# Regrouping an attention loop: four tensor bursts a batch instead of eight

## The chip, the cores and the metric

The kernel runs on one core of one Trainium2 chip. The metric is the device time of one execution in microseconds (us).

The engines are called TensorE (PE in the profile; PEld is its weight load), VectorE (DVE), ScalarE (ACT), GpSimd (POOL) and SyncE (SP).

## The reference

There are 32 batches of 512 x 512 floats and one 512 x 512 adjacency. Layer 0 is a graph sum with two weight matrices and a layer norm. Layer 1 is masked attention with 8 heads of 64 and a layer norm.

```
# layer 0
mi, mj = x @ Wi.T, x @ Wj.T
x = layernorm(x + deg * (mi + b) + adj @ mj)
# layer 1, 8 heads of 64
q, k, v = x @ Wq.T + bq, x @ Wk.T + bk, x @ Wv.T + bv
scores = q @ k.T / 8;  scores[adj == 0] = -inf
x = layernorm(x + (softmax(scores) @ v) @ Wo.T + bo)
```

## The kernel before

All matmuls of 512 columns in float32 show as two instructions. On the whole array one of these takes 0.43 us (eight in 3.43 us, from 2054.74 to 2058.17 in the trace of the kernel before); eight of the scores, two heads at once, take 1.92 us (2079.41 to 2081.33). Two heads form a pair (`hp`), four pairs make a batch, and the 512 keys are four blocks (`kc`). Scores use the upper and the lower half of the array for the two heads at once (64*128 in the profile), values and denominators its left and right half (128*64), everything else the whole array (128*128).

```
def scores(b, hp, kc):
    ps = sc_tile()                                   # PSUM, 2 tiles of 2 banks
    for s in range(2):                               # two heads, one in each row half
        nc.tensor.matmul(ps[:, s, :], KT..., QT..., start=True, stop=True)
    e = E[kc] = work([P, 2, N], "e", 4)
    nc.scalar.activation(e, ps, AF.Exp)
    nc.vector.tensor_tensor(e, e, edge..., op=OP.mult)        # the mask product
    ... nc.vector.tensor_add(ES[hp], ES[hp], e)               # sum over key blocks

def values(b, hp, half): ...   # E[kc] times V, two key blocks, into PV[hp]
def sums(b, hp): ...           # ones times ES: the denominators
def invert / scale: ...        # VectorE: reciprocal in two halves, check, OT = PV * rl
```

A burst of attention is such a run of scores, values and denominators with nothing between them. The other work of a batch is a list `todo` of pieces, which belong to the next batch's layer 0 and its q, k, v and to the last batch's projection. The loop puts it between the bursts of attention. In the traces VectorE and ScalarE work in the order in which the program issues it (kernel before, from 2079 to 2098 us).

```
for step in range(8):
    hp, half = divmod(step, 2)
    scores(b, hp, 2 * half); scores(b, hp, 2 * half + 1)
    values(b, <pair and half of the step before>)     # and sums(), if it was a second half
    ... an eighth of todo, with invert, invert, scale put between its pieces
```

Pieces:

```
def l0_gather(b, dc):              # four of them open a batch
    pt = mm_tile()                 # mm: two PSUM banks, shared by all pieces in turn
    ... 4 transposes of x into pt
    nc.vector.tensor_mul(XD[b][:, dc, :], pt, deg_r)
    pm = mm_tile()
    # x = xhi + xlo: xhi is cast by ScalarE, xlo = x - xhi comes from VectorE
    ... 4 matmuls of xhi, then 4 of xlo, into pm
    nc.scalar.copy(AX_T[b][:, dc, :], pm)

def l0_out(b, ic):                 # bias on VectorE, 8 matmuls, ln_apply(ic - 1), sum, statistics
def l0_norm(b, ic):                # 4 transposes of the normed rows, ScalarE takes them out
```

## Time and profile before

| | before |
|---|---|
| time, median of the 3 runs before the prediction | 4282.94 us (4280.12 to 4285.44) |
| TensorE busy | 97% |
| VectorE, ScalarE, GpSimd busy | 61%, 21%, 9% |
| granted TensorE clock, mean | 0.996 |
| first scores of batch 0 | 112.4 us after the start |
| batch 0, mean of batches 1 to 30, last batch | 121.95, 131.79, 94.87 us |

The last two rows are read from the start of the first scores of each batch. They add up to the span: 112.4 + 121.95 + 30 x 131.785 + 94.87 = 4282.8 us. A difference in the mean of batches 1 to 30 counts 30 times.

The view of waits of the kernel before, TensorE only (who waited, for whom, us in total, times, longest):

```profile
PE mm L205 <- DVE xlo L182: 32.4, 32, 3.9
PE mm L205 <- ACT l L211: 23.8, 93, 0.3
PE mm L246 <- DVE xh L224: 10.7, 31, 0.3
```

TensorE waits about 0.9 us a batch for xlo, three times 0.24 us for ScalarE's copies between the gathers, and 0.34 us for VectorE once before the v matmuls. These are its only regular waits.

### The profile page before, as it was taken

Reading aid. Unit: us, or ns where it says so; the run is one execution under the profiler, and the core shown is the slowest. Engines: PE = TensorE matmul, PEld = TensorE weight load, DVE = VectorE, ACT = ScalarE, POOL = GpSimd, SP = SyncE. Lnnn points to the kernel's source line nnn. Section 1 sums busy time; section 2 is a strip of 40 time slices with the busy share of each in tenths; the row PEclk is TensorE's granted clock in tenths of the full one; section 3 lists DMA queues with packets and bytes.
Section 4 is the critical chain, followed back from the end, with each engine's and each line's share of the span. In section 5 each row is a group of like instructions: output and inputs, shape, how many; then the busy total and the mean of one; then the engine's idle time right before and its main releaser. Section 6 shows DMA issues by size and latency. Waiting matters only on the chain.

```text
span 4282.8 us, 31600 instructions
## 1 busy us (share of the span) xinstructions
PE 4174.9 (97%) x12826; PEld 1789.9 (42%) x12826; DVE 2607.0 (61%) x3081; ACT 894.1 (21%) x1159; POOL 399.1 (9%) x654
## 2 busy tenths in 40 slices
PE   8999999999999999999999999999999999999997
PEld 4444444444444444444444444444444444444442
DVE  2566566666566655566656666656665556665667
ACT  1222221122212222212222112221222221222211
POOL 1010001100011000111000110001100011100011
PEclk9999999999999999999999999999999999999999
DMA  2000000000000000000000000000000000000000
GB/s 106 0 20 20 1 20 20 20 20 1 20 20 20 20 19 1 20 20 20 20 1 20 20 20 20 1 20 20 20 20 20 1 20 20 20 20 1 20 10 20
DMA packets 37941, 77.29 MB, mean 18 GB/s; under 512 B 1248, under 2 KB 1248, under 8 KB 37792
## 3 DMA queue, kind: packets, MB, share of 16 engines
q1 hardware_dynamic: 35376, 70.26, 4.7%
q10 hardware_dynamic: 2112, 4.19, 0.3%
q8 instruction: 101, 1.65, 0.2%
q0 software_dynamic: 304, 0.79, 0.1%
q14 instruction: 48, 0.39, 0.0%
HBM read 41.68 MB, written 33.55 MB: 18 GB/s over the span
## 4 chain that ended last, share of the span: by engine, by line
PE 91%; DVE 6%; ACT 2%; issue 1%; DMA 0%; POOL 0%; ACTq 0%
PE mm L220 21%; PE mm L262 11%; PE sc L273 11%; PE mm L246 10%; PE mm L254 10%; PE mm L318 10%; PE ov L290 9%; PE mm L205 6%; DVE e L277 2%; PE ov L297 2%; ACT l L211 1%; PE mm L236 1%; ACT e L276 1%; DVE es L280 1%; DVE xh L224 1%
## 5 line engine op out<-in xcount | busy, mean ns | idle before, releaser
L277 DVE TENSOR_TENSOR e<-e,edge 128x1024 f32<-128x1024 f32 x512 | 680.7, 1350 | 999.4 <-ACT e L276 999.4
L276 ACT ACTIVATE e<-sc 128x1024 f32<-128x1024 f32 x512 | 496.3, 1021 | 1551.4 <-PE sc L273 1551.4
L273 PE MATMUL sc<-q,k 64*128 64x512 f32 x2048 | 510.6, 617 | 0.0
L290 PE MATMUL ov<-e,v 128*64 128x512 f32 x2048 | 496.8, 605 | 6.3 <-DVE e L277 3.8
L262 PE MATMUL mm<-l,wk 128*128 128x512 f32 x1024 | 466.7, 599 | 0.0
L318 PE MATMUL mm<-wo,oT 128*128 128x512 f32 x1024 | 460.0, 602 | 5.6 <-DVE oT L311 5.6
L246 PE MATMUL mm<-wv,l 128*128 128x512 f32 x1024 | 453.7, 596 | 11.4 <-DVE xh L224 10.7
L220 PE MATMUL mm<-wi,l 128*128 128x512 f32 x1024 | 461.1, 593 | 1.7 <-DVE xh L224 1.0
L254 PE MATMUL mm<-l,wq 128*128 128x512 f32 x1024 | 460.5, 593 | 0.0
L220 PE MATMUL mm<-wj,l 128*128 128x512 f32 x1024 | 460.4, 592 | 0.0
L303 DVE RECIPROCAL rl<-ov 128x256 f32<-128x256 f32 x256 | 438.8, 1736 | 0.0
L168 POOL TENSOR_SCALAR mv<-mv 128x1 f32<-128x1 f32 x256 | 71.1, 278 | 3433.1 <-DVE mv L167 3433.1
L282 DVE TENSOR_TENSOR es<-es,e 128x1024 f32<-128x1024 f32 x256 | 313.6, 1225 | 8.8
L318 PEld LDWEIGHTS mm<-wo,oT 128*128 128x128 f32 x1024 | 190.1, 191 | 273.7 <-issue 217.7
L273 PEld LDWEIGHTS sc<-q,k 64*128 64x128 f32 x2048 | 176.9, 186 | 303.8 <-issue 302.2
L262 PEld LDWEIGHTS mm<-l,wk 128*128 128x128 f32 x1024 | 189.8, 190 | 264.9 <-issue 215.5
L254 PEld LDWEIGHTS mm<-l,wq 128*128 128x128 f32 x1024 | 194.8, 190 | 244.9 <-issue 244.9
L220 PEld LDWEIGHTS mm<-wj,l 128*128 128x128 f32 x1024 | 194.9, 190 | 244.6 <-issue 244.6
L246 PEld LDWEIGHTS mm<-wv,l 128*128 128x128 f32 x1024 | 189.7, 190 | 233.4 <-issue 213.5
L224 DVE TENSOR_TENSOR xh<-xh,mm 128x512 f32<-128x512 f32 x128 | 88.1, 688 | 322.1 <-PE mm L220 322.1
L220 PEld LDWEIGHTS mm<-wi,l 128*128 128x128 f32 x1024 | 189.7, 190 | 216.3 <-issue 213.4
L290 PEld LDWEIGHTS ov<-e,v 128*64 128x64 f32 x2048 | 124.3, 136 | 348.2 <-issue 263.0
(62 smaller groups left out, 2863.3 us busy)
## 6 DMA issues: line engine op xcount, KB each, us to landing
xh<-in_x_dram SPq DMA_DIRECT2D x32, 1024.0 KB, 5.2
out_dram<-xh SPq DMA_DIRECT2D x32, 1024.0 KB, 4.3
wj<-in_wjT_dram ACTq DMA_DIRECT2D x1, 1024.0 KB, 11.7
l<-in_adj_dram SPq DMA_DIRECT2D x1, 1024.0 KB, 9.6
wi<-in_wiT_dram ACTq DMA_DIRECT2D x1, 1024.0 KB, 16.7
wv<-in_wvT_dram SPq DMA_DIRECT2D x1, 1024.0 KB, 20.4
wk<-in_wkT_dram ACTq DMA_DIRECT2D x1, 1024.0 KB, 21.5
wq<-in_wqT_dram SPq DMA_DIRECT2D x1, 1024.0 KB, 25.2
```

The source lines that it names most:

```text
L205: nc.tensor.matmul(pm, parts[w][:, jc, :], adjR[:, jc, :], start=(w == 0 and jc == 0), stop=(w == 1 and jc == NC - 1))
L220: nc.tensor.matmul(pm, src[:, dc, ic * P:(ic + 1) * P], (wi, wj)[w][:, dc, :], start=(w == 0 and dc == 0), stop=(w == 1 and dc == DC - 1))
L246: nc.tensor.matmul(pm, HT[b][:, dc, ic * P:(ic + 1) * P], wv[:, dc, :], start=(dc == 0), stop=(dc == DC - 1))
L254: nc.tensor.matmul(pm, wq[:, dc, hp * P:(hp + 1) * P], HT[b][:, dc, :], start=(dc == 0), stop=(dc == DC - 1))
L262: nc.tensor.matmul(pm, wk[:, dc, hp * P:(hp + 1) * P], HT[b][:, dc, :], start=(dc == 0), stop=(dc == DC - 1))
L273: nc.tensor.matmul(ps[:, s, :], KT[b, hp][r, kc * P:(kc + 1) * P], QT[b, hp][r, :], start=True, stop=True)
L276: nc.scalar.activation(e, ps, AF.Exp)
L277: nc.vector.tensor_tensor(e, e, edge[:, kc:kc + 1, :].to_broadcast([P, 2, N]), op=OP.mult)
L282: nc.vector.tensor_add(ES[hp], ES[hp], e)
L290: nc.tensor.matmul(PV[hp][s * HD:(s + 1) * HD, :], V[b][:, kc, c0:c0 + HD], E[kc][:, s, :], start=(kc == 0), stop=(kc == NC - 1))
L303: nc.vector.reciprocal(rl[:, c], pl[:, c])
L318: nc.tensor.matmul(pm, OT[b, hp][:, ic * P:(ic + 1) * P], wo[:, hp, :], start=(hp == 0), stop=(hp == HP - 1))
```

## The change

Each change between array shapes (a switch) costs TensorE time, 0.171 us by run 4. The intent is to have fewer of them. A pair gets one burst: scores of half its keys, denominators and all values of the pair ahead, scores of the other half. To carry this, six exponential tiles are kept instead of four, and q, k and the key sums give back one tile each.

```diff
-        e = E[kc] = work([P, 2, N], "e", 4)
+        e = E[hp, kc] = work([P, 2, N], "e", 6)
...
-    def values(b, hp, half):
-        for kc in range(2 * half, 2 * half + 2):
+    def values(b, hp):
+        for kc in range(NC):
...
+    def rest(b, hp, extra):
+        sums(b, hp)
+        values(b, hp)
+        extra += [(invert, b, hp, 0), (invert, b, hp, 1), (scale, b, hp)]
...
-        for step in range(STEPS):
-                scores(b, hp, 2 * half)
-                scores(b, hp, 2 * half + 1)
-                ... values of the step before, sums at every second step
+        for hp in range(HP):
+                scores(b, hp, 0)
+                scores(b, hp, 1)
+                rest(*prev, extra)
+                scores(b, hp, 2)
+                scores(b, hp, 3)
                 ... then a quarter of todo (an eighth before)
```

More of the change, by code (lines that the diff above doesn't have):

```diff
@@ L250, in q_out @@
     def q_out(b, hp):
-        QT[b, hp] = work([P, N], "q", 6)
+        QT[b, hp] = work([P, N], "q", 5)
         pm = mm_tile()
@@ L258, in k_out @@
     def k_out(b, hp):
-        KT[b, hp] = work([P, N], "k", 6)
+        KT[b, hp] = work([P, N], "k", 5)
         pm = mm_tile()
@@ L278, in scores @@
         if kc == 1:
-            ES[hp] = work([P, 2, N], "es", 2)
-            nc.vector.tensor_add(ES[hp], E[0], E[1])
+            ES[hp] = work([P, 2, N], "es", 1)
+            nc.vector.tensor_add(ES[hp], E[hp, 0], e)
         elif kc > 1:
             nc.vector.tensor_add(ES[hp], ES[hp], e)
-    def values(b, hp, half):
-        if half == 0:
-            PV[hp] = ov_tile()
-        for kc in range(2 * half, 2 * half + 2):
+    def values(b, hp):
+        PV[hp] = ov_tile()
+        for kc in range(NC):
             for s in range(2):
                 c0 = hp * P + s * HD
-                nc.tensor.matmul(PV[hp][s * HD:(s + 1) * HD, :], V[b][:, kc, c0:c0 + HD], E[kc][:, s, :],
+                nc.tensor.matmul(PV[hp][s * HD:(s + 1) * HD, :], V[b][:, kc, c0:c0 + HD], E[hp, kc][:, s, :],
                                  start=(kc == 0), stop=(kc == NC - 1))
@@ L348, in run @@
         f[1](*f[2:])
+    def rest(b, hp, extra):
+        sums(b, hp)
+        values(b, hp)
+        extra += [(invert, b, hp, 0), (invert, b, hp, 1), (scale, b, hp)]
     for f in first(0) + second(0):
         run(f)
-    STEPS = 2 * HP
     for b in range(B + 1):
@@ L359, in gnn_attention_kernel @@
         total, done, at = sum(f[0] for f in todo), 0.0, 0
-        extra = []
-        for step in range(STEPS):
-            if b < B:
-                hp, half = divmod(step, 2)
-                scores(b, hp, 2 * half)
-                scores(b, hp, 2 * half + 1)
-                if step > 0:
-                    ph, phalf = divmod(step - 1, 2)
-                    values(b, ph, phalf)
-                    if phalf == 1:
-                        sums(b, ph)
-                        extra = [(invert, b, ph, 0), (invert, b, ph, 1), (scale, b, ph)]
-            if step == 0 and b > 0:
-                values(b - 1, HP - 1, 1)
-                sums(b - 1, HP - 1)
-                extra = [(invert, b - 1, HP - 1, 0), (invert, b - 1, HP - 1, 1), (scale, b - 1, HP - 1)]
-            if step == 5 and b + 2 < B:
+        for hp in range(HP):
+            extra = []
+            prev = (b, hp - 1) if hp > 0 else (b - 1, HP - 1)
+            if hp == 0 and b == B:
+                rest(*prev, extra)
+            if b < B:
+                scores(b, hp, 0)
+                scores(b, hp, 1)
+                if prev[0] >= 0:
+                    rest(*prev, extra)
+                scores(b, hp, 2)
+                scores(b, hp, 3)
+            if hp == 2 and b + 2 < B:
                 load_x(b + 2)
-            while at < len(todo) and done < total * (step + 1) / STEPS - 1e-6:
+            while at < len(todo) and done < total * (hp + 1) / HP - 1e-6:
                 while extra and todo[at][1] is proj:
@@ L389, in gnn_attention_kernel @@
                 g[0](*g[1:])
-            extra = []
         for f in todo[at:]:
```

## The prediction

> **What bounds the kernel now.** I read the page first, then TensorE (PE) in order of time for a middle batch, then VectorE (DVE) in the same stretch, then TensorE at the start, where the pipeline is not yet full.
>
> ```profile
> PE 4174.9 (97%) x12826; PEld 1789.9 (42%) x12826; DVE 2607.0 (61%) x3081; ACT 894.1 (21%) x1159; POOL 399.1 (9%) x654
> ```
>
> TensorE is busy 97% of the time, so its work and its gaps are the time; DVE at 61% matters only where TensorE waits for it. The change removes no arithmetic. It can gain from what TensorE spends between groups, and lose by new gaps. TensorE in order of time (start, length, engine, line, operation, operands, shape, count):
>
> ```profile
> 2046.55 1.99 PE L273 MATMUL sc<-q,k 64*128 64x512 f32 x8
> 2048.47 1.94 PE L290 MATMUL ov<-e,v 128*64 128x512 f32 x8
> 2050.24 1.03 PE L297 MATMUL ov<-es,ones 128*64 128x512 f32 x4
> 2051.20 3.70 PE L262 MATMUL mm<-l,wk 128*128 128x512 f32 x8
> 2054.74 3.60 PE L254 MATMUL mm<-l,wq 128*128 128x512 f32 x8
> ...
> 2079.41 1.99 PE L273 MATMUL sc<-q,k 64*128 64x512 f32 x8
> ...
> 2084.05 0.66 PE L194 MATMUL mm<-ident,xh 128*128 128x128 f32 x4
> 2084.47 1.18 PE L205 MATMUL mm<-adjR,xhi 128*128 128x512 f32 x4
> 2086.52 1.20 PE L205 MATMUL mm<-adjR,xlo 128*128 128x512 f32 x4 [0.87 <-DVE xlo L182]
> ```
>
> The first five lines price a switch between array shapes. Eight undisturbed full-array matmuls take 3.43 us (the q group starts at 2054.74, the next k group at 2058.17), 0.43 each. Scores (64*128) and values and denominators (128*64) run two at a time, so the 8, 8 and 4 of a burst need 4, 4 and 2 rounds: 1.72 + 1.72 + 0.86. With 3.43 for the k group that is 7.73; the trace has 8.19 from 2046.55 to 2054.74, and the q group ahead takes 3.52 instead of 3.43. So three switches (full to row halves, to column halves, to full) cost 0.55 us, **0.18 us each**.
>
> The last four lines are the start of a batch: after the burst the gather of the next batch's layer 0 begins, and its second part waits 0.87 us for a DVE product (xlo). DVE there, and in the step after:
>
> ```profile
> 2081.64 2.36 DVE L277 TENSOR_TENSOR e<-e,edge 128x1024 f32<-128x1024 f32 x2 [9.40 <-ACT e L276]
> 2084.04 1.23 DVE L280 TENSOR_TENSOR es<-e 128x1024 f32<-128x1024 f32 x1
> 2085.18 0.68 DVE L195 TENSOR_TENSOR l<-mm,deg_r 128x512 f32<-128x512 f32 x1
> 2085.78 1.28 DVE L182 TENSOR_TENSOR xlo<-xh,xhi 128x512 fp32r<-128x512 f32 x2
> ...
> 2098.34 1.23 DVE L277 TENSOR_TENSOR e<-e,edge 128x1024 f32<-128x1024 f32 x1 [3.80 <-ACT e L276]
> 2099.61 1.22 DVE L282 TENSOR_TENSOR es<-es,e 128x1024 f32<-128x1024 f32 x1
> 2100.75 1.22 DVE L277 TENSOR_TENSOR e<-e,edge 128x1024 f32<-128x1024 f32 x1
> ```
>
> The mask products and the key sums of a burst stand in DVE's queue ahead of the gather's xlo. Each product with its sum takes 2.40 us (2098.34 to 2100.75). The first starts 2.23 us after its scores; xlo is ready only 0.74 us after it starts at 2085.78.
>
> The start of the run is a rehearsal, because there the gather follows the scores with no values between:
>
> ```profile
> 112.44 1.99 PE L273 MATMUL sc<-q,k 64*128 64x512 f32 x8
> 114.35 0.66 PE L194 MATMUL mm<-ident,xh 128*128 128x128 f32 x4
> 116.11 1.19 PE L205 MATMUL mm<-adjR,xhi 128*128 128x512 f32 x4 [1.10 <-ACT xhi L181]
> 119.54 2.08 PE L205 MATMUL mm<-adjR,xlo 128*128 128x512 f32 x4 [2.24 <-DVE xlo L182]
> ```
>
> xlo starts 7.10 us after the scores, as in the middle batch (2086.52 - 2079.41 = 7.11), so DVE sets it. And the xlo group then takes 2.08 us where 1.20 is normal: in the windows view the granted clock is 0.50 from 119.5 to 124.2. The gap of 1.10 + 2.24 us with about 1 us of work inside put TensorE at half speed.
>
> [...] a gap of 3.04 us near the end (4195.4 to 4198.4) and one of 2.59 us were enough, and so was the broken one above; the trace's clock records put the falls at 118.7, 4197.6 and 4259.0 us, each for one or two periods of 3.41 us, and the periods that ended there held 25 to 35% of matmul work. [...] beside GpSimd's bias sum (2005.20) a mask product takes 2.29 us instead of 1.22.
>
> **The change, part by part.** The built order confirms the intent. A pair of heads had two bursts (scores of two key blocks, values of two, at the second also the denominators); it has one now: two score blocks, denominators and all values of the pair before, two score blocks. On DVE all four products and three sums now stand in one row ahead of whatever follows the burst.
>
> Switches: a pair had six, now four (full to rows, to columns, to rows, to full). 2 x 0.18 = 0.36; with the printed starts the old two bursts and the new one come to 8.82 and 8.48, so 0.34 us a pair. 128 pairs: **-43 us**. Matmul rounds, exponentials, products and reciprocals are unchanged in number. The buffers do not bind: the fifth exponential tile of a pair is six back, one key-sum tile is read by the denominators at about 2.9 us and rewritten at 4.6, q and k with five tiles wait for pairs long finished.
>
> New timetable of a burst, from its start T. Scores 1.92, then ten rounds of denominators and values: 4 in 1.77, 2 with the closing switch in 0.96, 4 more by 0.43 = 4.45. The second scores start at T+6.37, the burst ends at T+8.29. DVE: products and first sum until T+5.9, then idle; third product at 6.37 + 2.23 = 8.60, two times 2.40, free at **T+13.4, 5.1 us after TensorE has left the burst**. Before, it was free 1.1 us after the burst (2085.18 against 2084.05) or 3.3 us (2103.2 against 2099.9).
>
> *Pair 0* (gather next): XD at 13.4, xlo at 14.0, usable at 14.74. That is 6.45 us after the burst ends, against 2.47 before (2086.52 - 2084.05): +3.98. The chain behind it is the same as before. 30 batches x 3.98, and about 2.5 in batch 0 that already waited: **+122 us**.
>
> *Pair 0, clock*: the gap is now about 1.5 us for xhi (the last exponential ends near T+9.5, then the cast), 1.05 of matmul, 3.5 for xlo. Every period of 3.41 us that starts between T+8.6 and T+12.5 has under 1.2 us of work (35%), and one must start there, so each batch falls to half clock. At the start 6.0 us at half clock cost 2.3 us (119.54 to 125.75, against 3.89 for the same groups from 2086.52). An average over phases of about 2.0: 30 x 2.0 = **+60 us**.
>
> *Pair 1* (last projection, two l0_out, then the first norm): DVE does 3.4 + 1.2 us of reciprocals and scaling first, the projection's sum at T+18.0, four ln_apply, then out0's sum at 22.3; ln_apply for norm0 ends near 25.9, TensorE is there at 25.7, and the next out waits for the sum behind it. About 0.6: 30 x 0.6 = **+18 us**.
>
> *Pair 2* (norm1, out3, norm2): GpSimd's bias sum now falls on DVE's products (+1.07), so DVE is free at 14.5; reciprocal 1.67, 0.65, ln_apply 0.55 end at 17.4. TensorE wants norm2 at 8.29 + 0.49 + 6.87 = 15.65. Wait 1.85, against 0.2 saved behind it: 31 x 1.65 = **+51 us**.
>
> *Pair 3* (q and k, evicted by ScalarE): nothing. The last batch, bound by DVE, changes little.
>
> Sum: 4283 - 43 + 122 + 60 + 18 + 51 = 4491.
>
> **Rivals.** *The switches decide*: DVE's 39% of idle time absorbs the bunching, the time is 4283 - 43 = 4240. Against it: the idle time lies elsewhere, and xlo is a short-notice consumer. *Only the wait, no clock fall*: windows land kindly and the pair 2 collision is off; 4283 - 43 + 122 + 30 = 4390. [...] against it, three of three such gaps fell. *The clock falls in pair 2 as well*: a window there has about 40% work, between the 35% that fell and the 56% that did not (2.24 us busy from 4248 to 4252, clock 1.00); 31 x 2 more gives 4550.
>
> **Range and chances.** The pair 0 wait rests on measured pitches; the clock and pair 2 terms are each good to about half. Predicted 4490 us, range 4410 to 4560. The 2% line is at 4369, which the pair 0 wait alone does not pass (4283 - 43 + 122 = 4362), so slower by over 2% gets 0.87, within 2% 0.10, faster 0.03.
>
> **What would show it.** Scores, denominators and values, scores in about 8.3 us; TensorE waiting some 3.5 us for xlo and 1.5 for xhi in each batch; half clock in the slice after it, 30 times; a wait of 1 to 2 us before the third norm. If xlo waits under 1.5 us, or the clock stays full through these gaps, or DVE's row ends before T+11, the prediction is wrong at that step.

The 0.18 us a switch, the falls and their grid of 3.41 us, and the 2.29 us of a mask product beside GpSimd's sum were read from the trace of the kernel before. That a period which holds about 35% of work or less ends in a fall is the author's estimate from three falls.

## The result

| | before | after |
|---|---|---|
| time, median of 4 runs | 4282.58 us (4280.12 to 4285.44) | 4504.85 us (4503.04 to 4505.35) |
| ratio | 1 | 1.0518 (95%: 1.05 to 1.0536) |
| granted clock, mean | 0.996 | 0.976 |
| falls to half clock in batches 1 to 30 | 0 | 30 |
| batch 0, mean of batches 1 to 30, last batch | 121.95, 131.79, 94.87 us | 122.26, 138.80, 103.75 us |

Ratios here and below are the mean time of one kernel's runs over that of the other's in the same rounds, so they are not quite the ratios of the medians. The change made the kernel 5.2% slower. The first column has one run more than the table further up, so its median differs. Of the 220 us by which the traced span grew, 30 x 7.02 = 211 are in the middle batches and 9 in the last one.

The page's first section and the view of waits of the changed kernel:

```profile
PE 4234.6 (94%) x12826; PEld 1848.5 (41%) x12826; DVE 2611.0 (58%) x3081; ACT 891.1 (20%) x1159; POOL 418.6 (9%) x654
PE mm L206 <- DVE xlo L183: 113.8, 32, 4.8
PE mm L237 <- DVE xh L173: 44.2, 31, 1.5
PE mm L206 <- ACT xhi L182: 36.5, 32, 2.6
PE mm L206 <- ACT l L212: 15.3, 64, 0.2
PE ov L297 <- DVE told L309: 12.9, 3, 5.7
```

The instruction counts are the same and VectorE's busy time hardly moved. TensorE's busy time grew by 60 us although it does the same work. That goes with the half clock (0.50 from 2192.50 to 2197.20 us), at which a group counts 2.08 us of busy time and not 1.20: in run 1 below, which has no fall in batches 1 to 30, TensorE is busy for 4164.2 us. TensorE in order of time at the start of a middle batch (start, length, engine, line, operation, operands, array shape, size, count; in brackets the idle time just before and what ended it):

```profile
2180.67 3.60 PE L290 MATMUL ov<-e,v 128*64 128x512 f32 x16
2184.20 1.99 PE L274 MATMUL sc<-q,k 64*128 64x512 f32 x8
2186.12 0.66 PE L195 MATMUL mm<-ident,xh 128*128 128x128 f32 x4
2187.88 1.20 PE L206 MATMUL mm<-adjR,xhi 128*128 128x512 f32 x4 [1.10 <-ACT xhi L182]
2192.57 2.08 PE L206 MATMUL mm<-adjR,xlo 128*128 128x512 f32 x4 [3.50 <-DVE xlo L183]
2194.45 1.05 PE L195 MATMUL mm<-ident,xh 128*128 128x128 f32 x4
2195.38 2.08 PE L206 MATMUL mm<-adjR,xhi 128*128 128x512 f32 x4
```

The burst ends at 2186.12 and xlo starts at 2192.57, 6.45 us later; before, this distance was 2.47. From 2192.57 on the groups take 2.08 us instead of 1.20. The windows view gives the clock for it (stretch, its length, then busy time of PE, PEld, DVE, ACT and POOL, the granted clock, DMA):

```profile
2186.20:2192.50 6.30, 1.77 (x8) 1.01 (x8) 5.99 (x7) 2.15 (x4) 0.00 (x0) 0.87 0.00 0
2192.50:2194.40 1.90, 1.83 (x4) 1.39 (x5) 1.90 (x3) 0.00 (x0) 0.00 (x0) 0.50 0.00 0
```

VectorE is busy for 5.99 of the first 6.30 us, while TensorE works 1.77. VectorE in order of time in the same burst:

```profile
2182.54 1.23 DVE L281 TENSOR_TENSOR es<-e 128x1024 f32<-128x1024 f32 x1
2186.44 1.23 DVE L278 TENSOR_TENSOR e<-e,edge 128x1024 f32<-128x1024 f32 x1 [2.67 <-ACT e L277]
2187.70 1.22 DVE L283 TENSOR_TENSOR es<-es,e 128x1024 f32<-128x1024 f32 x1
2188.84 1.22 DVE L278 TENSOR_TENSOR e<-e,edge 128x1024 f32<-128x1024 f32 x1
2190.09 1.23 DVE L283 TENSOR_TENSOR es<-es,e 128x1024 f32<-128x1024 f32 x1
2191.24 0.68 DVE L196 TENSOR_TENSOR l<-mm,deg_r 128x512 f32<-128x512 f32 x1
2191.84 1.28 DVE L183 TENSOR_TENSOR xlo<-xh,xhi 128x512 fp32r<-128x512 f32 x2
```

VectorE is idle for 2.67 us in the middle of the burst, because the second scores have not come yet. Then two products and two sums, 4.8 us, stand ahead of xlo. They are not needed before the next burst, whose scores start at 2214.38, 28 us after this burst has ended. TensorE needs xlo at once. The same happens on a smaller scale in pair 2:

```profile
2257.95 2.17 DVE L283 TENSOR_TENSOR es<-es,e 128x1024 f32<-128x1024 f32 x1
2264.67 0.54 DVE L173 TENSOR_SCALAR xh<-xh,mv 128x512 f32<-128x512 f32 x1
2265.36 0.63 PE L237 MATMUL mm<-ident,xh 128*128 128x128 f32 x4 [1.46 <-DVE xh L173]
```

Here a sum takes 2.17 us instead of 1.22; it stands beside GpSimd's bias sum (2257.12 to 2259.05 in the trace). The ln_apply (L173) comes after VectorE's row, and the third norm's transposes wait 1.46 us for it.

### The profile page after: what moved, and what is told of

It is laid out like the page before. It is cut to its first block, busy times and chain, and to the rows that moved or that the text cites. A ratio compares the mean times of both kernels' runs of the same rounds, so it can differ in the third digit from the quotient of the medians.

```text
span 4502.7 us, 31600 instructions
## 1 busy us (share of the span) xinstructions
PE 4234.6 (94%) x12826; PEld 1848.5 (41%) x12826; DVE 2611.0 (58%) x3081; ACT 891.1 (20%) x1159; POOL 418.6 (9%) x654
## 4 chain that ended last, share of the span: by engine, by line
PE 72%; DVE 21%; ACT 3%; issue 2%; POOL 2%; DMA 0%; DVEq 0%
PE mm L247 10%; PE mm L263 10%; PE ov L290 10%; PE mm L255 10%; PE sc L274 9%; PE mm L318 7%; PE mm L206 7%; PE mm L221 6%; DVE e L278 5%; DVE es L283 5%; DVE rl L303 4%; PE ov L297 3%; ACT e L277 2%; DVE xh L173 1%; DVE st L167 1%
## 5 line engine op out<-in xcount | busy, mean ns | idle before, releaser
L278 DVE TENSOR_TENSOR e<-e,edge 128x1024 f32<-128x1024 f32 x512 | 614.8, 1221 | 1064.8 <-ACT e L277 1064.8
L290 PE MATMUL ov<-e,v 128*64 128x512 f32 x2048 | 462.4, 593 | 0.0
L169 POOL TENSOR_SCALAR mv<-mv 128x1 f32<-128x1 f32 x256 | 82.9, 324 | 3697.0 <-DVE mv L168 3697.0
L283 DVE TENSOR_TENSOR es<-es,e 128x1024 f32<-128x1024 f32 x256 | 343.0, 1340 | 8.8
L206 PE MATMUL mm<-adjR,xlo 128*128 128x512 f32 x512 | 180.0, 483 | 113.8 <-DVE xlo L183 113.8
L238 ACT COPY l<-mm 128x512 f32<-128x512 f32 x128 | 75.2, 588 | 1018.9 <-PE mm L237 1018.9
```

Of the source, the lines that this page charges most:

```text
L206: nc.tensor.matmul(pm, parts[w][:, jc, :], adjR[:, jc, :], start=(w == 0 and jc == 0), stop=(w == 1 and jc == NC - 1))
L278: nc.vector.tensor_tensor(e, e, edge[:, kc:kc + 1, :].to_broadcast([P, 2, N]), op=OP.mult)
L290: nc.tensor.matmul(PV[hp][s * HD:(s + 1) * HD, :], V[b][:, kc, c0:c0 + HD], E[hp, kc][:, s, :], start=(kc == 0), stop=(kc == NC - 1))
```

## The experiments

Each run was timed beside the kernel before on the same chip, three or five rounds; all outputs were correct. A fall is a clock record at half clock. In the traces of the kernels before and after (5 and 36 falls in the whole run) the falls start on one grid of 3.4133 us, to within 0.001 us, and "period" means a step of this grid. "Changed kernel" is the kernel after the change.

### 1. VectorE's order alone

```diff
-                scores(b, hp, 2)
-                scores(b, hp, 3)
+                late = hp == 0 and b + 1 < B        # issue only matmuls and Exp
+                scores(b, hp, 2, late)
+                scores(b, hp, 3, late)
...
+                if b + 1 < B and hp == 0 and at == DC:   # after the four gathers
+                    mask(hp, 2)
+                    mask(hp, 3)
```

> The changed kernel, TensorE's order untouched; only on VectorE the third and fourth mask product of pair 0, with their sums, are issued after the four gathers instead of ahead of them. Theory (the row of products ahead of xlo costs the wait, and the wait costs the clock): TensorE's wait for xlo falls from 3.5 us a batch to under 0.3, the 1.1 us for xhi stays, the clock stays full in the steady batches, and the time falls by 31 x 3.5 + about 60 to some 4335 us. Rival (TensorE's new order itself, its buffers or its switches cost the time): the time stays within 20 us of 4505.

Measured: 4333.38 us (4332.51 to 4334.58), ratio 1.012 to the kernel before. No fall of the clock is left in batches 1 to 30 (mean granted clock 0.996). The view of waits:

```profile
PE mm L237 <- DVE xh L173: 44.2, 31, 1.5
PE mm L206 <- ACT xhi L182: 36.5, 32, 2.6
PE mm L206 <- DVE xlo L183: 4.3, 1, 4.3
```

The wait for xlo is gone from all batches but one, at the start of the run, with TensorE's order untouched. So 171 us hang on where VectorE's four instructions stand, and on what follows from it. Some 28 of them are a wait for xlo that the kernel before has too (32.4 us in its view, 4.3 here), so about 143 us are of the loss. The rival falls.

### 2. The gap filled with useless work

```diff
             parts = SPLIT.pop((b, dc))
+            if dc == 0 and b > 0:
+                for _ in range(18):                 # overwritten: the next matmul starts pm anew
+                    nc.tensor.matmul(pm, adjR[:, 0, 0:P], adjR[:, 1, :], start=True, stop=True)
```

> The changed kernel with 18 useless matmuls a batch (0.26 us each, 4.7 us in all) put into the gap in which TensorE waits for xhi and xlo; their result is overwritten. Theory (the gap throws the clock to half, and that costs some 2 us a batch beyond the wait): the added work lies in the gap, the clock stays full, and the kernel gets faster by about 60 us, to some 4445. Rival (the half clock costs nothing because VectorE sets the pace of the gathers): no change within 10 us, or slower by up to 30 x 4.7 = 141 us if the gap is not really free.

Measured: 4452.22 us (4451.33 to 4452.85), so 52.6 us faster than the changed kernel with 558 matmuls more (18 in each of 31 batches). TensorE in order of time:

```profile
2160.63 0.66 PE L195 MATMUL mm<-ident,xh 128*128 128x128 f32 x4
2161.04 4.38 PE L206 MATMUL mm<-adjR 128*128 128x512 f32 x18
2165.26 1.09 PE L209 MATMUL mm<-adjR,xhi 128*128 128x512 f32 x4
2167.08 1.21 PE L209 MATMUL mm<-adjR,xlo 128*128 128x512 f32 x4 [0.73 <-DVE xlo L183]
```

xlo starts 6.45 us after the burst as in the changed kernel, so the added work (18 matmuls in 4.22 us) lay wholly in the gap. The groups behind it take 1.21 us and not 2.08, the clock in the stretches from 2160.6 to 2171.0 is 1.00, and no fall is recorded in batches 1 to 30. A middle batch is 137.04 us long instead of 138.80. So the half clock by itself costs 1.77 us a batch, 53 us in all, on top of the wait. This run separates the two.

### 3. Half of the filling

```diff
-                for _ in range(18):
+                for _ in range(9):
```

> As the run that filled the gap, with 9 useless matmuls a batch instead of 18: the wait for xhi is filled, a single wait for xlo of about 2.8 us stays. If a period of 3.41 us has to hold under about 35% of work for the clock to fall, a gap of 2.8 us makes it fall in about half of the batches: some 15 falls beyond the 7 of the filled run, and some 4452 + 30 = 4480 us. If any gap of that length is enough, 30 falls and 4505; if it takes the broken gap, none and 4452.

Measured: 4480.05 us (4478.1 to 4481.85). The time is as expected, but by two errors that cancel. The clock fell in 23 of the 30 middle batches, not in 15 (mean granted clock 0.986, and 0.995 in run 2), and each fall lasted one period of 3.41 us, where 20 of the 30 falls of the changed kernel lasted two. A fall therefore cost (137.88 - 137.04) x 30 / 23 = 1.1 us instead of 1.77. The clock records fix the period's grid, so the share of matmul work in each period can be counted: all 23 periods that ended in a fall held at most 44% of work, and of the periods in the middle batches that did not end in one, the emptiest held 46.5%. For these gathers the limit lies between, and not at the 35% that the prediction had taken from three cases. It is no rule for all work: in the last batches of run 6 and run 5 a period with 41% and one with 42%, with nothing but scores in it, did not end in a fall. Busy time is modelled at its ends, and what the clock really counts stays open.

### 4. The switches alone

The kernel before, with the second half of the values put behind the first piece of other work, in 187 places.

```diff
-                    values(b, ph, phalf)
+                    values(b, ph, phalf, (0,))          # one key block in the burst
...
                 run(todo[at])
+                if split_v:
+                    values(*split_v)                    # the other behind the first piece
```

> The kernel before, with values split in 187 places round the first piece of other work: the second key block's two matmul rounds move behind it, so that 374 array-shape switches are added and no work. Theory (0.18 us a switch): +67 us, some 4350. Rival (a switch costs nothing, the excess in the starts is a reading artefact): within 10 us of 4283. If switches cost twice as much, +135.

Measured: 4345.76 us (4345.55 to 4347.79), the kernel before in the same rounds 4281.72. 64.0 us for 374 switches is 0.171 us a switch; the traces have 764 switches before and 1138 here, and the waits hardly moved (xlo 32.1 us against 32.4). So the price that the prediction read from the starts is real. The changed kernel has 512 switches, and 252 less are worth 43 us. A first form of this run, which split the values at every step, was refused before the chip, because VectorE would have read values in the middle of their accumulation; the record does not hold it.

### 5. The wait in pair 2

```diff
+                if hp == 2 and b > 0 and b + 1 < B:
+                    l0_ready(b + 1, 3)     # bias of out3 and ln_apply(2), in VectorE's idle time
                 scores(b, hp, 2)
```

> The changed kernel with two short VectorE operations of pair 2 (the bias of out3 and the ln_apply that norm2 needs) issued between the first and the second scores, into VectorE's idle 2.7 us. Theory: the 1.46 us that TensorE waits for norm2 in 30 batches goes, the rest stays: 4505 - 44 = some 4460. Rival (that wait is only a symptom and comes back behind, as a wait for out3's sum): within 10 us of 4505.

Measured: 4467.76 us (4464.98 to 4468.32), 37 us less than the changed kernel. The wait for ln_apply is gone from the view of waits, and the view has a new entry behind it:

```profile
PE mm L257 <- DVE xh L235: 13.8, 31, 0.5
```

The rival holds in part: of the 44 us, 13.8 came back as a wait for out3's sum, which stands next on VectorE. Between starts, the wait was 1.62 us a batch where the bracket in the timeline says 1.46, and 0.55 came back; the rest of the 37 us (1.62 - 0.55 is 1.07 a batch, 32 us) are small shifts that I did not follow.

### 6. The burst of pair 0 undone

```diff
+                late = hp == 0 and b + 1 < B      # then issued after the four gathers
+                if not late:
                     scores(b, hp, 2)
                     scores(b, hp, 3)
```

> The changed kernel with one part undone for pair 0 alone: its second scores come after the four gathers, as a burst of their own, so that only two products and one sum stand ahead of xlo. It adds two array-shape switches in 31 batches (31 x 2 x 0.171, as measured, = 11 us). Theory: both waits of the gather (1.1 and 3.5 us) and the half clock go: 4505 - 31 x 4.6 - 60 + 11 = some 4313. Rival (the merged burst itself costs, for instance through the exponential tiles): above 4400.

Measured: 4324.87 us (4322.31 to 4325.92). The clock stays full in the middle batches (mean over the run 0.995) and the waits for xhi are gone, but the view of waits still has 19.2 us for xlo, 0.44 us in a middle batch: VectorE has no row ahead of it any more, but it has to take out the transposes before it makes xlo, and without the wait for xhi this shows. That is about the 12 us by which the expectation was missed. The theory holds: one burst of four, undone, brings back 180 of the 222 us; as in run 1, a part of that, here some 13 us (32.4 - 19.2), is a wait that the kernel before has too.

### 7. The row hidden, and its control

Two kernels. The first keeps the four bursts, holds back the last q and k of a batch and puts them between burst 0 and the gathers; reciprocals and the ln_apply of pair 2 go into VectorE's idle time. The control is the kernel before with only q and k held back.

```diff
+        todo = held(b) if 0 < b < B else []           # q_out(b, 3), k_out(b, 3)
+        todo = todo + (first(b + 1) if b + 1 < B else [])
...
+            todo = todo + second(b + 1)[:-2]
```

> The four bursts kept, and VectorE's row hidden: the last q and k of a batch (whose results ScalarE takes out) are held back and put between burst 0 and the gathers, 6.9 us of TensorE work that needs no VectorE; the first reciprocal and, in pair 2, the bias and ln_apply go into VectorE's idle time inside the burst. Theory: no long wait is left, the clock stays full, the 43 us of saved switches show, and the 0.95 us a batch that the kernel before loses at the gather goes too: 4283 - 43 - 28, plus some 10 for the first and the last batch = some 4225, faster than both. Rival (the bunched row only moves the wait to the next consumer): 4283 or more.

> The kernel before with only the last q and k of a batch held back and put ahead of the gathers, its eight bursts kept. A control for the run above: theory: the 0.95 us a batch at the gather go, 4283 - 28 = some 4255, so that the four bursts themselves are worth some 30 us once their row is hidden. Rival (holding q and k back is all the gain, four bursts are worth nothing): the same time as the run above within 10 us.

Measured: 4281.55 us (4280.52 to 4283.15) and 4280.53 us (4280.45 to 4281.11), the kernel before in the same rounds 4284.08. Both expectations failed, by 57 and by 26 us. The long waits and the half clock are gone from the middle batches of the first kernel (mean granted clock 0.996), yet neither is faster than the kernel before beyond the noise (ratios 0.9996 and 0.9994, intervals 0.998 to 1.0009). TensorE of the first kernel in order of time, at the gathers and at a norm:

```profile
2084.41 3.60 PE L273 MATMUL mm<-l,wk 128*128 128x512 f32 x8
2087.84 0.60 PE L195 MATMUL mm<-ident,xh 128*128 128x128 f32 x4
2089.29 1.19 PE L206 MATMUL mm<-adjR,xhi 128*128 128x512 f32 x4 [0.85 <-ACT xhi L182]
2151.40 0.60 PE L247 MATMUL mm<-ident,xh 128*128 128x128 f32 x4
2152.34 3.70 PE L231 MATMUL mm<-wi,l 128*128 128x512 f32 x8 [0.34 <-DVE xh L235]
```

The wait for xlo has made room for a wait for xhi: ScalarE takes out the held k first and casts x after it. The k group ends at 2088.01 (a modelled end); with 0.69 us to take it out and 0.62 for the cast (means of the kernel before) xhi should start at 2089.32, an estimate, and it starts at 2089.29. That happens in both kernels (29.0 and 29.1 us of waits for xhi in all). In the first, three of the four norms also stand between two groups of matmuls with no burst next to them, where before one did. A norm is 0.5 us of transposes in one of the two mm banks, and the group after it needs the bank that was filled just before the norm, which VectorE has yet to empty. So 1.4 us of saved switches and 1 us of saved xlo waits are spent on other waits.

### 8. The transposes in banks of their own, and the control

The score banks are idle outside a burst. Both kernels send the transposes there and issue the first split of x early; the first is the kernel with the hidden row, the second the kernel before.

```diff
-        pt = mm_tile()
+        pt = sc_tile()[:, 0, :]        # in l0_gather and in l0_norm
...
+                if hp == 0 and b > 0 and b + 1 < B:
+                    split(b + 1, 0)
```

> The run with the hidden row was 4282 us and not 4225: per batch its switches are 1.3 us cheaper than before, but TensorE now waits 0.85 us for ScalarE's cast xhi (queued behind the held k) and 0.34 us at each of three norms, because the short transposes take one of the two mm banks in turn and the next matmul group needs the bank just filled. Here the transposes go to the score banks, which are idle outside a burst, and the first split of x is issued inside burst 0. Expected: 131.7 - 1.0 - 0.8 (the waits for ScalarE's copies between gathers) - 1.2 = some 128.7 us a batch, 4282 - 90 = some 4190 us, faster than the kernel before by 2%. Rival (other waits take their place): 4240 or more.

> The control: the kernel before, eight bursts, with the same two remedies (transposes into the score banks, the first split issued early) and no held q and k. It should lose its 0.95 us at the gather, the 0.8 us between gathers and 0.35 at v: 4283 - 30 x 2.1 = some 4220 us. If four bursts are worth their 1.3 us of switches a batch once nothing waits, the run above is faster than this one by 25 to 40 us; if not, the two are equal within 10.

Measured: 4148.84 us (4148.01 to 4149.57), ratio 0.9686 (0.9673 to 0.9699), and 4176.57 us (4174.34 to 4177.47), ratio 0.975 (0.9737 to 0.9764). Both beat the kernel before by over 2%, and the first beats all others. With four bursts:

```profile
2020.78 0.60 PE L195 MATMUL sc<-ident,xh 128*128 128x128 f32 x4
2021.14 1.18 PE L206 MATMUL mm<-adjR,xhi 128*128 128x512 f32 x4
2022.15 1.10 PE L206 MATMUL mm<-adjR,xlo 128*128 128x512 f32 x4
2023.09 0.60 PE L195 MATMUL sc<-ident,xh 128*128 128x128 f32 x4
2089.32 0.60 PE L247 MATMUL sc<-ident,xh 128*128 128x128 f32 x4
2089.76 7.03 PE L257 MATMUL mm<-wv,l 128*128 128x512 f32 x16
```

No wait is left at these places. Both gained about 42 us more than expected, because the expectation added up the bracketed waits. From transposes to xhi is 0.36 us here and was 0.84 in the kernel before, so the loss was 0.48 us a gather, while the bracket had said 0.24. From the first transposes of the gathers to the burst behind them the kernel before takes 12.06 us and its control here 9.38, a gain of 2.68 where the brackets add up to 1.64; over 30 batches the difference is 31 us. A bracket counts from a modelled end of the matmul before; the distance between starts has it all.

The two differ by 27.7 us, inside the 25 to 40 us expected, so the four bursts are worth something once nothing long waits. It is less than the 43 us of their switches: the first kernel still has 8.4 us of waits, in 31 batches, before a norm whose score bank ScalarE has yet to empty. The pair is not quite pure, since the first also holds q and k back, places reciprocals and an ln_apply early, and has another last batch (99.6 us against 93.6); its middle batches are 0.93 us shorter (127.57 against 128.49).

## Why the prediction was right

The forecast was 4490 us with a range of 4410 to 4560; it came to 4504.85. By its steps, in the order of its sum:

| step | predicted | measured | from |
|---|---|---|---|
| switches | -43 us | -43 | run 4: 252 x 0.171 |
| pair 0, wait | +122 | +120 | xlo 6.45 us after the burst, as worked out: 30 x 3.98, and 0.3 in batch 0 |
| pair 0, clock | +60 | +53 | run 2: 30 x 1.77 |
| pair 1 | +18 | +21 | starts: 0.7 us more between burst 1 and burst 2 |
| pair 2 | +51 | +52 | starts: 1.7 us more from norm1 to the last v |
| last batch | 0 | +9 | starts: 94.87 to 103.75 us |

The measured terms add up to 212 us of the 220 by which the span grew; some 8 us are spread over small shifts that I did not follow. Runs 1, 2, 4, 5 and 6 bear on the switches, pair 0 and pair 2; the terms of pair 1 and of the last batch are read from starts alone. The sum of pair 2 has a slip: 17.4 - 15.65 is 1.75 us and not 1.85, so the term should have been 48 us. The measured wait was 1.62.

**The row on VectorE** was the right mechanism, and xlo starts 6.45 us after the burst as predicted. Run 1 shows that it is the order on VectorE and not the one on TensorE, and run 6 shows the same from the other side.

**The clock** was right in kind and size, with one premise off. The prediction said that each batch must fall, which it did, 30 times of 30. The share of work that it named as the limit, 35%, was only what three falls happened to hold; run 3 puts the limit for its gathers between 44% and 46.5%. For the changed kernel this made no difference, since the periods that ended in its 30 falls held 2% to 35%. The half clock lasted one period in 10 of these falls, where that period held 88% to 95% of work, and two in the other 20, where the first held 46% to 79% and the second all.

**The last batch** was the step that failed. "Changes little" was argued from VectorE being the bound there before and after. Its busy time hardly moves (72.4 us before, 72.9 after), but TensorE's bursts also wait for each other through VectorE: the waits view has 12.9 us in three waits for the denominators' PSUM tile, and one of 7.0 us for the first projection, against 2.5 us and 5.6 us (two waits) in the kernel before. No run here isolates this, so the cause of the 9 us stays open.

**Batch 0** was to lose 2.5 us and lost 0.3. I did not follow why; that this offsets a part of the last batch is luck.

**The rivals.** "The switches decide" is refuted by run 1: the switches are cheaper, as it says, and VectorE's idle 2.67 us do not help, because they lie ahead of the scores that the row waits for. "Only the wait, no clock fall" is refuted by the clock records. "The clock falls in pair 2 as well" did not occur: all 30 falls in batches 1 to 30 belong to the gathers, one a batch, and the emptiest of the other periods at full clock held 57% of work.

## What to carry to other kernels

When TensorE is the bound and matmuls are regrouped, write down for each engine that feeds it which instructions the new order puts ahead of the next thing TensorE needs; here the work in front counted (4.8 us ahead of xlo) and not the engine's share of busy time (58%). A wait on TensorE that left a 3.41 us period of these gathers with at most 44% of matmul work (2% to 35% in the changed kernel, up to 44% in run 3) had to be priced twice, as the wait and as the half clock after it (120 and 53 us in the changed kernel). Useless matmuls in the gap bought the second part back when they filled most of it (52.6 us, run 2), and only half of it when they filled less (24.8 us, run 3). Before moving a wait, look at which queue and which PSUM bank the next consumer stands in: here two fixes came to nothing (run 7, ratios 0.9996 and 0.9994) until the short transposes had banks of their own and x was split early (run 8, 0.9686 and 0.975); the two remedies were not tried apart.
